# Moving adds and copies between engines in a pipelined Mamba block: D x and down's residual on TensorE, post-norm steps re-timed

## The chip, the cores and the metric

The kernel runs on one core of a Trainium2 chip. [...] An instruction waits at the head of its engine's queue until the semaphores that it names have come, and what is behind it waits too. Everything is 32-bit floating point. The metric is device time in microseconds (us) of one execution; lower is better.

## The reference

The input x has 4 sequences of 1024 rows of 256 values. Two layers follow each other, each with a layer norm in front and a residual sum behind it.

```
x = x + L0_attn(layernorm(x))      # a Mamba block with its own MLP
x = x + L0_ffn(layernorm(x))       # a gated FFN with a Walsh-Hadamard transform

L0_attn(h0):                                       # h0 = layernorm(x)
    z, x1, B, C, dt_raw = split(rmsnorm(h0) * n1 @ in_proj.T)  # 256, 64, 64, 256, 128 columns
    dt = softplus(dt_raw @ dt_proj.T + bias)
    state[g,p,n] = exp(dt*A) * state + (dt*x1) * B   # per time step: 256 rows (g,p), 32 states n
    y[g,p]       = sum_n state[g,p,n] * C[g,n]
    y = (y + D * x1) * silu(z)
    h = h0 + y @ out_proj.T
    return h + (silu(xn @ gate.T) * (xn @ up.T)) @ down.T      # xn = rmsnorm(h) * n2; 704 wide
L0_ffn(h1):                                        # h1 = layernorm(x after the first layer)
    return fwht(silu(h1 @ W1.T) * (h1 @ W3.T)) @ W2.T          # 1024 wide
```

## The kernel before

**Units and quarters.** The 4 x 1024 rows are cut into eight units of 512 rows (`T`), two to a sequence; unit 2k starts with an empty state ("even" units), unit 2k+1 goes on from the state that its predecessor left ("odd" units). For the scan, a unit has 256 rows x 32 states = 8192 recurrences over 512 time steps. They are worked on 128 partitions in 16 portions of four 512-long rows each, called q (0 to 127 over all units; `qs`, L696). For one q:

- SP issues `da` (dt copied over the states, 1 MB, L704 by `dma_da`) into one of four buffers, two halves of `ub` (dt*x1, 512 KB each), and for every second q `cr` (C, 256 KB);
- ACT turns da into exp(dt*A) in four instructions (`exp`, L741);
- DVE multiplies ub by B (`times_b`, L765, two instructions) and runs the recurrence (`scan`, L774, four instructions of 512 steps);
- POOL multiplies the states by C (`times_c`, L784, one instruction over 4 x 512; in even units it first copies the last state out, L783);
- PE sums over states (`sum_states`, L795, four matmuls) into the PSUM bank `py`, of which there is one; eight q fill it. Only then is the da buffer free, and the da of q+4 can be issued into it.

`pb`, a PSUM copy of B that times_b reads, is renewed every eight q by `copy_b` (L754).

**Ticks.** The order of every queue is written out by hand. Half a q is a tick; a unit is 32 ticks. `at(tick, lane, fn)` puts a step on a lane of a tick, and the loop at L858 records each tick's lanes in a fixed order: PE, ACT, times_b, ACTb, two exp of the next q, a scan, DVE, the other scan, POOL0, times_c, POOL, sum_states, PEend, ACTend, SP, the loads, SPend. No time is attached to a tick: it says only what stands ahead of what on each engine. "ACT" stands ahead of a tick's exponentials and "ACTend" behind them.

**What runs beside the scan.** `pre(u, H)` makes a unit's operands ahead of its first tick H: first norm (`row_stats`, `small`, `un`), transposes, the projection by `win` (x1/B, dt, C, z), and the DMAs that lay dt, dt*x1, C and x1 out in HBM. `post(u, E, other)` does the rest behind its last tick E: y = py + D x1 by DVE (`y_dx`, L810), times silu(z) by POOL (`y_z`, L815), out_proj (`add_rows`, L306), the second norm, the MLP's three pairs of products (`gated`, L245: matmuls, silu and `up` copies on ACT, product on POOL) and `down`, the third norm, the FFN's products and its output product with `w2h`. So while unit k is scanned, unit k-1 goes through `post` and unit k+1 through `pre`. Behind tick 256 there is no scan left, and the last units' `post` is all that runs (the tail).

`add_rows` adds a product to the residual `hr` in one of two ways: DVE adds PSUM to hr (L316: down's, and all three in the last unit), or ACT copies PSUM out (`evict`, L321) and POOL adds (L325: out_proj and w2h of the other units). `dense_psum` hands out four PSUM banks in turn to everything that is not py, pb or bx.

## Time and profile before

| what | us |
|---|---|
| median of 3 runs | 1163.14 (1161.78 to 1168.64) |
| the profiled execution: its own time | 1173.07 |
| its span on the core | 1171.2 |
| first scan begins, last scan ends | 22.07, 1053.61 |
| busy in that stretch (22 to 1053.6): DVE, PE, POOL, ACT | 949.4, 838.7, 839.0, 739.3 |
| behind it (1053.6 to 1171.2): PE, DVE, POOL, ACT | 104.1, 4.9, 36.1, 34.6 |
| share of the 16 DMA engines busy in the two | 0.87, 0.03 |

Times by unit, from the first scan of one to the first scan of the next, are 138.0, 126.4, 130.1, 128.2, 128.1, 128.6, 125.5 and (to the last scan's end) 126.6 us. The page of a profile gives busy times, a chain of work followed back from the end, and groups of instructions by source line; each idle time is put down to the semaphore that came last. A line such as L226 or L306 is that of a helper and serves several steps, which the names of the tiles tell apart (out<-in: `dense<-xt,w` is the FFN's first products, `dense<-ht,wg` the MLP's, `dense<-w2h,g` the output product). A 32-bit matmul stands in the trace as two records, so `x16` of L226 is eight matmuls of 512 columns.

### The profile page before, as it was taken

The page shows a single profiled execution, that of the slowest core. Times are in us where ns is not written, and L with a number is a line of the kernel's source. Part 1 is how long each engine was busy: PE and PEld are TensorE (multiplying, and loading weights), DVE is VectorE, ACT ScalarE, POOL GpSimd, SP SyncE. Part 2 cuts the span into 40 slices and gives each one's busy share as a digit, 9 for nine tenths or more (in the row PEclk, how much of TensorE's full clock was granted, in tenths as well). Part 3 has the DMA queues.
Part 4 walks back from the last instruction along what each step waited for, and adds up shares of the span by engine and source line. Part 5 has one row for each costly group of instructions (what it writes and reads, how often), then busy time and mean ns, then how long its engine had stood idle before and what let it go on. Part 6 is the DMA issues. An engine that isn't in the chain of part 4 may idle for free.

```text
span 1171.2 us, 11883 instructions
## 1 busy us (share of the span) xinstructions
PE 959.6 (82%) x3374; PEld 456.5 (39%) x3374; DVE 962.9 (82%) x840; ACT 782.2 (67%) x1411; POOL 887.1 (76%) x515
## 2 busy tenths in 40 slices
PE   8464236969998799969996999979997987799978
PEld 3121012423634255423633364424543362336535
DVE  4897799999998989999999899999999899990000
ACT  3835556868768786779677786878685967563331
POOL 6675758878978888878977998789977898674312
PEclk9777558979899799979998899979997999789989
DMA  7989999898799889997799889988799789730000
GB/s 252 352 300 351 353 327 308 311 325 296 250 340 320 300 298 320 319 327 281 270 348 325 281 300 334 319 325 297 270 310 360 281 291 343 262 111 1 18 0 18
DMA packets 89441, 321.89 MB, mean 275 GB/s; under 512 B 9312, under 2 KB 20000, under 8 KB 73120
## 3 DMA queue, kind: packets, MB, share of 16 engines
q1 hardware_dynamic: 87520, 318.38, 77.1%
q10 hardware_dynamic: 1856, 2.75, 0.7%
q8 instruction: 27, 0.44, 0.1%
q14 instruction: 38, 0.31, 0.1%
HBM read 302.22 MB, written 18.87 MB: 274 GB/s over the span
## 4 chain that ended last, share of the span: by engine, by line
PE 25%; DMA 7%; DVE 6%; POOL 6%; issue 5%; ACT 4%; DVEq 0%; POOLq 0%; ACTq 0%; SPq 0%
PE dense L226 14%; PE dense L306 8%; DMA da<-dtd 5%; POOL da L784 4%; DVE da L774 3%; DVE bx L765 3%; PE py L795 3%; DMA ub<-ud 2%; ACT da L741 1%; POOL m L274 1%; POOL g L274 1%; DVE hr L316 0%; ACT up L270 0%; ACT L741 0%; ACT junk L173 0%
## 5 line engine op out<-in xcount | busy, mean ns | idle before, releaser
L784 POOL TENSOR_TENSOR da<-da,cr 128x2048 f32<-128x2048 f32 x128 | 580.0, 4531 | 86.8 <-DVE da L774 22.5
L741 ACT ACTIVATE da<-da,nega 128x512 f32<-128x512 f32 x508 | 334.4, 713 | 170.8 <-DMA da<-dtd 159.3
L774 DVE TENSOR_TENSOR_SCAN da<-da,carry,bx 128x512 f32<-128x512 f32 x256 | 315.7, 1268 | 20.0 <-DVE bx L765 7.6
L774 DVE TENSOR_TENSOR_SCAN da<-da,bx 128x512 f32<-128x512 f32 x256 | 300.2, 1209 | 37.0 <-ACT da L741 21.3
L765 DVE TENSOR_TENSOR bx<-ub,pb 128x1024 f32<-128x1024 f32 x254 | 312.2, 1229 | 20.3 <-ACT pb L754 9.3
L795 PE MATMUL py<-da,rsel 128*32 128x512 f32 x1024 | 162.5, 712 | 159.4 <-POOL da L784 159.4
L226 PE MATMUL dense<-xt,w 128*128 128x512 f32 x512 | 238.4, 621 | 1.4 <-ACT si L263 1.4
L226 PEld LDWEIGHTS dense<-xt,w 128*128 128x128 f32 x512 | 99.4, 199 | 145.9 <-issue 123.4
L795 PEld LDWEIGHTS py<-da,rsel 128*32 128x32 f32 x1024 | 21.4, 115 | 243.0 <-POOL da L784 201.2
L306 PE MATMUL dense<-w2h,g 128*128 128x256 f32 x512 | 113.4, 380 | 0.0
L274 POOL TENSOR_TENSOR g<-si,up 128x512 f32<-128x512 f32 x64 | 80.5, 1272 | 32.3 <-ACT up L270 32.2
L306 PEld LDWEIGHTS dense<-w2h,g 128*128 128x128 f32 x512 | 96.8, 190 | 18.4 <-ACT ev L321 2.5
L306 PE MATMUL dense<-wd,m 128*128 128x256 f32 (+1 forms) x384 | 98.2, 400 | 0.9 <-POOL m L274 0.9
L316 DVE TENSOR_TENSOR hr<-hr,dense 128x512 f32<-128x512 f32 x20 | 13.4, 669 | 99.9 <-PE dense L306 99.9
L226 PE MATMUL dense<-ut,win 128*128 128x512 f32 x192 | 94.7, 625 | 0.2 <-ACT ut L220 0.2
L270 ACT COPY up<-dense 128x512 f32<-128x512 f32 x112 | 63.4, 579 | 46.8 <-PE dense L226 46.4
L274 POOL TENSOR_TENSOR m<-si,up 128x512 f32<-128x512 f32 (+1 forms) x48 | 60.2, 1270 | 43.5 <-ACT up L270 43.5
L226 PE MATMUL dense<-ht,wg 128*128 128x512 f32 x192 | 87.7, 600 | 3.4 <-ACT ht L220 3.4
L306 PEld LDWEIGHTS dense<-wd,m 128*128 128x128 f32 (+1 forms) x384 | 68.6, 192 | 37.6 <-issue 20.6
L263 ACT ACTIVATE si<-dense 128x512 f32<-128x512 f32 x112 | 60.7, 596 | 28.4 <-PE dense L226 25.5
L226 PE MATMUL dense<-ht,wu 128*128 128x512 f32 x160 | 72.8, 600 | 4.8 <-ACT si L263 4.8
L741 ACT ACT_TABLE_LOAD x44 | 56.5, 1283 | 4.8 <-DMA da<-dtd 4.0
(95 smaller groups left out, 798.6 us busy)
## 6 DMA issues: line engine op xcount, KB each, us to landing
da<-dtd SPq DMA_DIRECT2D x127, 1024.0 KB
ub<-ud SPq DMA_DIRECT2D x254, 512.0 KB
cr<-cd SPq DMA_DIRECT2D x64, 256.0 KB
x<-in_x SPq DMA_DIRECT2D x8, 512.0 KB
dtd<-dt SPq DMA_DIRECT2D x16, 256.0 KB
ud<-du SPq DMA_DIRECT2D x16, 256.0 KB
cd<-cc SPq DMA_DIRECT2D x16, 256.0 KB
out<-hr SPq DMA_DIRECT2D x8, 512.0 KB
```

The lines of the kernel that those rows point to most:

```text
L226: nc.tensor.matmul(dst[:n], lhsT=w[:, k, col : col + n], rhs=src[:, k, :], start=(k == 0), stop=(k == 1),)
L263: nc.scalar.activation(g[i]["si"][:n], g[i]["pg"][:n], AF.Silu)
L270: nc.scalar.copy(g[i]["up"][:n], g[i]["pu"][:n])
L274: nc.gpsimd.tensor_tensor(u[dst][:n, c, :], g[i]["si"][:n], g[i]["up"][:n], ALU.mult)
L306: nc.tensor.matmul(po[t // 2][:, t % 2, :], lhsT=left[k][:, t * P : (t + 1) * P], rhs=right[k], start=(k == 0), stop=(k == n - 1),)
L316: nc.vector.tensor_tensor(hr, hr, po[i], ALU.add)
L741: nc.scalar.activation(da, da if q else s["u"]["pdt", b], AF.Exp, scale=an[:, s["h"], s["j"], b, s["g"] : s["g"] + 1],)
L765: nc.vector.tensor_tensor(s["bx"], s["ub", b0 // 2], u["pb"].unsqueeze(1).broadcast_to([P, 2, T]), ALU.mult)
L774: nc.vector.tensor_tensor_scan(da, da, s["bx"][:, b % 2, :], start, ALU.mult, ALU.add)
L784: nc.gpsimd.tensor_tensor(s["da"], s["da"], s["cr"].unsqueeze(1).broadcast_to([P, 4, T]), ALU.mult)
L795: nc.tensor.matmul(u["py"][32 * b : 32 * b + 32, :], lhsT=rsel[:, 2 * s["j"] + s["g"], :], rhs=s["da"][:, b, :], start=first, stop=last,)
```

## The change

- **D x on TensorE.** `diagonal` makes two 128x128 diagonal matrices of D (`dd`, by ACT, once). `sum_states` starts each py with a matmul of dd and x1's rows (`xr`), 16 in all. `y_dx` on DVE becomes a copy of py by ACT, behind the exponentials of the same tick (ACTend); for the last half of the last unit DVE multiplies py by silu(z) straight away (`y_z_last`).
- **The rows behind down on TensorE.** `add_rows` with way "pe" starts each of down's four row blocks with a matmul of the identity and hr (32 in all); the sum is then copied back over hr by ACT (in the last unit, the second half by DVE) where DVE added it. Unit 6's out_proj, so far by ACT and POOL, goes the DVE way, and its w2h keeps POOL's.
- **copy_b** goes to ACT in 13 of 15 cases (7 before); DVE keeps q = 8 and 120.
- **Steps moved.** In units 0 to 5 all of `post` from the second norm's `hn` on is a tick later (F = E+1), and the third norm's `hn` stands behind the exponentials. In units 6 and 7 it is sooner: 2 ticks for the second norm and the MLP's first products (F = E-2), 3 to 5 for down and its statistics, 5 behind the third norm. `down` runs two row blocks to a tick there. Unit 6's four w2h blocks are at E+32, E+36 and twice E+50, which is, on PE's queue, ahead of unit 7's out_proj, behind it, and behind unit 7's down. In `pre`, `un` and the transposes are two ticks later (units 2 to 7), and the x1, dt and first C projections with the DMAs of x1 and B one tick later (units 1 to 7).
- **gated**: where z's matmul rides along, the first `up` copy stands behind the exponentials and the first product a tick later.
- **The end**: the last times_c is cut in two, the first half a tick sooner; unit 7's m and g lie in da's buffers instead of the one "big" buffer; the last half of its statistics is DVE's (`row_stats_vector`); its rows are stored in two halves.

```diff
     rsel = load("rsel", [P, 8, 32], a["rsel"])
+    dd = wp.tile([P, 2, P], F32, tag="dd", name="dd")
+    def diagonal(h):
+        nc.scalar.activation(dd[:, h, :], ident, AF.Identity, scale=dpar[:, h : h + 1])
...
-    def row_stats_first(u, src):
-        u["mv"] = sm.tile([P, 2, TT], F32, tag="mv", name="mv")
-        st = sm.tile([P, TT, 6], F32, tag="st", name="st")
-        ag = sm.tile([P, TT, 2], F32, tag="ag", name="ag")
-        for t in range(TT):
+    def row_stats_vector(u, name, ts=range(TT)):
+        src = u[name]
+        if 0 in ts:
+            u["mv"] = sm.tile([P, 2, TT], F32, tag="mv", name="mv")
+        st = p1.tile([P, TT, 6], F32, tag="st", name="st")
+        ag = p1.tile([P, TT, 2], F32, tag="ag", name="ag")
+        for t in ts:
             nc.vector.bn_stats(st[:, t, :], src[:, t, :])
-        for t in range(TT):
+        for t in ts:
             nc.vector.bn_aggr(ag[:, t, :], st[:, t, :])
-        nc.vector.tensor_copy(u["mv"][:, 1, :], ag[:, :, 1])
-        nc.vector.tensor_scalar(u["mv"][:, 0, :], ag[:, :, 0], -1.0 / 16, None, ALU.mult)
+        ts = slice(ts[0], TT)
+        nc.vector.tensor_copy(u["mv"][:, 1, ts], ag[:, ts, 1])
+        nc.vector.tensor_scalar(u["mv"][:, 0, ts], ag[:, ts, 0], -1.0 / 16, None, ALU.mult)
...
             c, n = chunks[i]
-            nc.gpsimd.tensor_tensor(u[dst][:n, c, :], g[i]["si"][:n], g[i]["up"][:n], ALU.mult)
+            nc.gpsimd.tensor_tensor(u[dst][c][:n], g[i]["si"][:n], g[i]["up"][:n], ALU.mult)
...
         at(tick + 1, "ACTend" if three else "ACT", silus)
-        at(tick + 2, "ACT", up, 0)
+        at(tick + 2, "ACTend" if z else "ACT", up, 0)
...
                 at(tick + 2, "ACTend", up, i)
-        at(tick + 2, "POOL", product, 0)
+        at(tick + 3 if z else tick + 2, "POOL", product, 0)
...
             at(tick + 3, "POOL", product, i)
-    def add_rows(tick, u, lhs, rhs, per_tick, lane="PE", on_pool=False):
+    def add_rows(ticks, u, lhs, rhs, lane="PE", way=None):
...
             n = len(left)
+            dst = po[t // 2][:, t % 2, :]
+            if way == "pe":
+                rows = u["hr"][:, t, :]
+                nc.tensor.matmul(dst, lhsT=ident, rhs=rows, start=True, stop=False)
...
                 nc.tensor.matmul(
-                    po[t // 2][:, t % 2, :],
+                    dst,
...
                     rhs=right[k],
-                    start=(k == 0),
+                    start=(k == 0 and way != "pe"),
...
             nc.vector.tensor_tensor(hr, hr, po[i], ALU.add)
+        def replace(i):
+            copy = nc.vector.tensor_copy if by_vector(i) else nc.scalar.copy
+            copy(u["hr"][:, 2 * i : 2 * i + 2, :], po[i])
+        def by_vector(i):
+            return u is us[-1] and i
...
         for t in range(TT):
-            at(tick + t // per_tick, lane, pe, t)
+            at(ticks[t], lane, pe, t)
             if t % 2:
-                after = tick + t // per_tick + 1
-                if on_pool:
+                after = ticks[t] + 1
+                if way == "pe":
+                    at(after, "DVE" if by_vector(t // 2) else "ACTend", replace, t // 2)
+                elif way == "pool":
...
             at(H - 54, "SP", load_x, u)
-            at(H - 45, "ACTend", lambda: row_stats(u, u["x"], (0, 1)))
-            at(H - 43, "ACTend", lambda: row_stats(u, u["x"], (2, 3)))
+            at(H - 45, "ACTend", row_stats, u, "x", (0, 1))
+            at(H - 43, "ACTend", row_stats, u, "x", (2, 3))
...
             at(H - 37, "POOL", small_end)
-            at(H - 32, "ACT", un, (0, 1))
-            at(H - 31, "ACT", un, (2, 3))
-            at(H - 30, "PE", lambda: transposes(u, s["un"]))
-            at(H - 30, "ACTend", transposed, u, "ut")
-        at(H - 24, "PE", pe_x)
-        at(H - 23, "ACT", act_x)
-        at(H - 22, "SP", dma_xb)
-        at(H - 19, "SPend", dma_xr, 0)
-        at(H - 17, "SPend", dma_xr, 1)
-        at(H - 16, "PE", pe_dt)
-        at(H - 16, "PE", pe_c, 0)
+            at(H - 30, "ACT", un, (0, 1))
+            at(H - 29, "ACT", un, (2, 3))
+            at(H - 28, "PE", lambda: transposes(u, s["un"]))
+            at(H - 28, "ACTend", transposed, u, "ut")
+        at(H - 23, "PE", pe_x)
+        at(H - 22, "ACT", act_x)
+        at(H - 21, "SP", dma_xb)
+        at(H - 18, "SPend", dma_xr, 0)
+        at(H - 16, "SPend", dma_xr, 1)
+        at(H - 15, "PE", pe_dt)
+        at(H - 15, "PE", pe_c, 0)
...
         s = {}
+        last = u is us[-1]
+        many = us.index(u) < len(us) - 2
...
         def big(name):
-            u[name] = p1.tile([P, 8, T], F32, tag="big", name=name)
-        def store():
-            b, c = u["b"], u["c"]
+            if last:
+                tiles = [pda.tile([P, 4, T], F32, tag="da", name=name) for _ in range(2)]
+                u[name] = [tiles[c // 4][:, c % 4, :] for c in range(8)]
+            else:
+                tile = p1.tile([P, 8, T], F32, tag="big", name=name)
+                u[name] = [tile[:, c, :] for c in range(8)]
+        def store(lo=0, n=TT):
+            b, first = u["b"], u["c"] * T + lo * P
             nc.sync.dma_start(
-                out=out[b, c * T : (c + 1) * T, :].rearrange("(t p) d -> p t d", p=P), in_=u["hr"]
+                out=out[b, first : first + n * P, :].rearrange("(t p) d -> p t d", p=P),
+                in_=u["hr"][:, lo : lo + n, :],
...
         add_rows(
-            E + 3,
+            (E + 3,) * TT,
...
             lambda: [W["wo"][:, k, :] for k in range(2)],
-            4,
             "PEend",
-            on_pool=u is not us[-1],
+            way="pool" if many else None,
         )
-        at(E + 5, "ACTend", lambda: row_stats(u, u["hr"], (0, 1), False))
-        at(E + 6, "ACTend", lambda: row_stats(u, u["hr"], (2, 3), False))
-        at(E + 7, "POOL", small2)
-        at(E + 8, "ACT", hn, "r3", None)
-        at(E + 9, "PE", lambda: transposes(u, s["tok"]))
-        at(E + 9, "ACTend", transposed, u, "ht")
-        at(E + 9, "POOL", lambda: nc.gpsimd.tensor_tensor(u["hr"], u["hr"], u["x"], ALU.add))
-        at(E + 10, "PE", big, "m")
+        for i in range(2):
+            at(E + (5 + i if many else 4), "ACTend", row_stats, u, "hr", (2 * i, 2 * i + 1), False)
+        F = E + 1 if many else E - 2
+        at(E + 7 if many else E + 5, "POOL", small2)
+        at(F + 8, "ACT", hn, "r3", None)
+        at(F + 9, "PE", lambda: transposes(u, s["tok"]))
+        at(F + 9, "ACTend", transposed, u, "ht")
+        at(F + 9, "POOL", lambda: nc.gpsimd.tensor_tensor(u["hr"], u["hr"], u["x"], ALU.add))
+        at(F + 10, "PE", big, "m")
...
         for i in range(2):
-            gated(E + 10 + 3 * i, u, "m", "wg", "wu", chunks[3 * i : 3 * i + 3], "ht",
+            gated(F + 10 + 3 * i, u, "m", "wg", "wu", chunks[3 * i : 3 * i + 3], "ht",
                   (other, i) if other else None)
+        down = (18, 19, 20, 21) if many else (17, 17, 18, 18)
         add_rows(
-            E + 18,
+            [F + t for t in down],
             u,
-            lambda: [u["m"][:n, c, :] for c, n in enumerate(sizes)],
+            lambda: [u["m"][c][:n] for c, n in enumerate(sizes)],
             lambda: [W["wd"][:n, c, :] for c, n in enumerate(sizes)],
-            1,
+            way="pe",
         )
-        at(E + 20, "ACTend", lambda: row_stats(u, u["hr"], (0, 1)))
-        at(E + 22, "ACTend", lambda: row_stats(u, u["hr"], (2, 3)))
-        at(E + 23, "POOL", small3)
-        at(E + 24, "ACT", hn, "r4", "nm")
-        at(E + 25, "PE", lambda: transposes(u, s["tok"]))
-        at(E + 25, "ACTend", transposed, u, "xt")
-        at(E + 26, "PE", big, "g")
+        at(F + down[1] + 1, "ACTend", row_stats, u, "hr", (0, 1))
+        if last:
+            at(F + down[3] + 1, "DVE", row_stats_vector, u, "hr", (2, 3))
+        else:
+            at(F + down[3] + 1, "ACTend", row_stats, u, "hr", (2, 3))
+        at(F + down[3] + 2, "POOL", small3)
+        if not many:
+            F -= 3
+        at(F + 24, "ACTend" if many else "ACT", hn, "r4", "nm")
+        at(F + 25, "PE", lambda: transposes(u, s["tok"]))
+        at(F + 25, "ACTend", transposed, u, "xt")
+        at(F + 26, "PE", big, "g")
...
         for i in range(3):
-            gated(E + 26 + 3 * i, u, "g", "w1", "w3", chunks8[3 * i : 3 * i + 3], "xt")
+            gated(F + 26 + 3 * i, u, "g", "w1", "w3", chunks8[3 * i : 3 * i + 3], "xt")
+        o2 = (E + 32, E + 36, E + 50, E + 50) if not (many or last) else range(F + 36, F + 40)
         add_rows(
-            E + 36,
+            o2,
             u,
-            lambda: [u["g"][:, c, :] for c in range(8)],
+            lambda: u["g"],
             lambda: [w2h[:, c, :] for c in range(8)],
-            1,
-            on_pool=u is not us[-1],
+            way=None if last else "pool",
         )
-        at(E + 43, "SPend", store)
+        if last:
+            at(o2[1] + 1, "SPend", store, 0, 2)
+            at(o2[3] + 1, "SPend", store, 2, 2)
+        else:
+            at(o2[3] + 4, "SPend", store)
...
         return s["u"]["carry"][:, s["h"], s["j"], :, s["g"]]
+    def by_vector(q):
+        return q in (8, NQ - 8)
...
         u["pb"] = ps_b.tile([P, T], F32, tag="b", name="pb")
-        (nc.vector.tensor_copy if h else nc.scalar.copy)(u["pb"], u["br", h])
+        (nc.vector.tensor_copy if by_vector(q) else nc.scalar.copy)(u["pb"], u["br", h])
...
         nc.vector.tensor_tensor_scan(da, da, s["bx"][:, b % 2, :], start, ALU.mult, ALU.add)
-    def times_c(q):
+    def times_c(q, parts=(slice(0, 4),)):
...
             nc.gpsimd.tensor_copy(carry_of(s), s["da"][:, :, T - 1])
-        nc.gpsimd.tensor_tensor(
-            s["da"], s["da"], s["cr"].unsqueeze(1).broadcast_to([P, 4, T]), ALU.mult
-        )
+        for part in parts:
+            da = s["da"][:, part, :]
+            n = da.shape[1]
+            nc.gpsimd.tensor_tensor(
+                da, da, s["cr"].unsqueeze(1).broadcast_to([P, n, T]), ALU.mult
+            )
...
             u["py"] = ps_y.tile([P, T], F32, tag="y", name="py")
+            x = u["xr"][:, s["h"], :]
+            nc.tensor.matmul(u["py"], lhsT=dd[:, s["h"], :], rhs=x, start=True, stop=False)
...
                 rhs=s["da"][:, b, :],
-                start=first,
+                start=False,
...
         if last:
-            at(2 * q + 4, "DVE", y_dx, u, s["h"])
-            at(2 * q + 5, "POOL0", y_z, u, s["h"])
-    def y_dx(u, h):
+            if q == NQ - 1:
+                at(2 * q + 4, "DVE", y_z_last, u)
+            else:
+                at(2 * q + 4, "ACTend", y, u, s["h"])
+                at(2 * q + 5, "POOL0", y_z, u, s["h"])
+    def y(u, h):
...
             u["yt"] = p3.tile([P, 2, T], F32, tag="T", name="yt")
-        nc.vector.scalar_tensor_tensor(
-            u["yt"][:, h, :], u["xr"][:, h, :], dpar[:, h : h + 1], u["py"], ALU.mult, ALU.add
-        )
+        nc.scalar.copy(u["yt"][:, h, :], u["py"])
...
         nc.gpsimd.tensor_tensor(u["yt"][:, h, :], u["yt"][:, h, :], u["zs"][:, h, :], ALU.mult)
+    def y_z_last(u):
+        nc.vector.tensor_tensor(u["yt"][:, 1, :], u["py"], u["zs"][:, 1, :], ALU.mult)
...
     at(-17, "ACTend", weights_ready)
+    for h in range(2):
+        at(1, "ACTend", diagonal, h)
...
         at(2 * q - 8, "SPend", dma_br, q)
-        at(2 * q - 1, "DVE" if q // 8 % 2 else "ACTb", copy_b, q)
+        at(2 * q - 1, "DVE" if by_vector(q) else "ACTb", copy_b, q)
...
         run(tick, "POOL0")
-        if half == 0 and has(q - 1):
+        if half == 0 and has(q - 1) and q < NQ:
             times_c(q - 1)
+        elif q in (NQ - 1, NQ) and tick >= 2 * NQ - 1:
+            if tick <= 2 * NQ:
+                times_c(NQ - 1, (slice(0, 2) if half else slice(2, 4),))
```

## The prediction

> **What bounds the kernel now.** I read the page's first part, then busy times by stretch, then VectorE's queue in order of time, then the waits, then the tail. First the page, and the two stretches into which the last scan cuts the span (columns: length, busy us and instructions of each engine, granted clock of TensorE, share of the DMA engines, GB/s).

> ```profile
> span 1171.2 us, 11883 instructions
> ...
> PE 959.6 (82%) x3374; PEld 456.5 (39%) x3374; DVE 962.9 (82%) x840; ACT 782.2 (67%) x1411; POOL 887.1 (76%) x515
> ...
> 22.00:1053.60 1031.60, 838.70 (x2993) 386.78 (x2995) 949.38 (x805) 739.28 (x1326) 839.01 (x460) 0.89 0.87 306
> 1053.60:1171.20 117.60, 104.14 (x348) 62.10 (x340) 4.89 (x8) 34.63 (x75) 36.05 (x29) 0.97 0.03 9
> ```

> While scans run, DVE is busy 949 of 1032 us; behind them it is idle and TensorE works 104 of 118 us. These are two regimes and I add them up apart. That DVE sets the pace of the first shows in its queue, here two ticks of unit 7:

> ```profile
> 1006.35 1.23 DVE L765 TENSOR_TENSOR bx<-ub,pb 128x1024 f32<-128x1024 f32 x1
> 1007.67 1.28 DVE L774 TENSOR_TENSOR_SCAN da<-da,carry,bx 128x512 f32<-128x512 f32 x1
> 1008.87 0.66 DVE L316 TENSOR_TENSOR hr<-hr,dense 128x512 f32<-128x512 f32 x1
> 1009.44 1.27 DVE L774 TENSOR_TENSOR_SCAN da<-da,carry,bx 128x512 f32<-128x512 f32 x1
> 1010.75 1.23 DVE L765 TENSOR_TENSOR bx<-ub,pb 128x1024 f32<-128x1024 f32 x1
> 1012.09 2.45 DVE L774 TENSOR_TENSOR_SCAN da<-da,carry,bx 128x512 f32<-128x512 f32 x2
> 1014.57 1.23 DVE L765 TENSOR_TENSOR bx<-ub,pb 128x1024 f32<-128x1024 f32 x1
> ```

> No line names a wait. The tick with an add takes 4.40 us, the next 3.82: an add costs the scan 0.58, its 0.66 less some overlap. But the others are close, as units 2 (even) and 3 (odd) show:

> ```profile
> 286.50:416.60 130.10, 115.42 (x407) 56.01 (x406) 117.16 (x101) 96.88 (x177) 109.74 (x70) 0.91 0.87 300
> 416.60:544.80 128.20, 116.67 (x427) 55.24 (x427) 120.96 (x101) 100.42 (x183) 109.04 (x54) 0.95 0.89 314
> ```

> DVE is busy 117 and 121 us, PE 115 and 117. An even unit has shorter scans (1209 ns against 1268 with a carry), so there the rest must hurry, and there DVE loses 13 us. Where it waits, and what SP waits for:

> ```profile
> DVE hr L316 <- PE dense L306: 99.9, 6, 43.9
> ...
> DVE yt L810 <- PE py L795: 12.5, 7, 8.9
> ...
> DVE bx L765 <- ACT pb L754: 9.3, 3, 4.1
> ...
> SPq L704 <- PE py L795: 286.2, 95, 7.3
> ```

> The first is nearly all tail, as is 8.9 us of the second. The fourth is the ring: the da of q+4 is issued when PE has summed q, so a late PE delays an exponential four q on. In unit 2 the margin between exponential and scan falls from 9.7 us (q 32) to nothing (q 39).

> **DVE's work that goes (scan stretch).** y_dx: 15 of the 16 stand there, at 733 ns less the same 0.09 overlap: 15 x 0.64 = 9.6, and 12.5 - 8.9 = 3.6 of waiting for py, which moves to ACT. copy_b: 6 at 674 ns, 6 x 0.58 = 3.5. Adds: 14 of down go, 2 for unit 6's out_proj come: 12 x 0.58 = 7.0. **Sum 23.7 us.**

> **A stall that should go.** At the end of units 2, 4 and 6 DVE waits 9.3 us for pb. ACT's queue tells why (unit 2's end):

> ```profile
> 412.38 0.60 ACT L263 ACTIVATE si<-dense 128x512 f32<-128x512 f32 x1 [0.63 <-PE dense L226]
> 414.09 0.58 ACT L270 COPY up<-dense 128x512 f32<-128x512 f32 x1 [1.11 <-PE dense L226]
> 414.58 0.60 ACT L754 COPY pb<-br 128x512 f32<-128x512 f32 x1
> ```

> pb stands behind silu and an up copy of the FFN's second product group, which wait for a late PE. A tick later (F = E+1) both stand behind pb. What is late next is PE's first group; the gain lies between 0 and 9.3, I take **6**, since one group less stands ahead of it.

> **TensorE's additional work.** The FFN's 512-column matmuls run at 16 records in 7.13 us, 0.89 for a matmul; the 256-column ones of w2h at 64 records in 13.98, 0.44. So 16 x 0.89 + 32 x 0.44 = 28.3 us, 26.5 of it in the scan stretch, 3.5 a unit: PE 119 to 120 us against a unit of some 124. It is free where PE waits for POOL ahead of py (159.4 us in all in the group of L795) and goes into the ring where PE is behind. The first matmul of a py also waits until ACT has emptied the one bank. Today py of q 48 could start when its times_c ended at 427.7; the exponentials of q 50, behind which the copy will stand, began at 427.4, so with 1.33 for two, 0.58 and 0.89 it starts at 430.2, 2.5 late; at q 40 it is 0.6, at q 120 nothing. ACT gets 15 + 15 + 6 copies of 0.58 = 21 us more, in 28 to 33 us of idle time a unit. Against all this, the first `up` copy no longer holds exponentials (at 337.34 it waited 2.13 us for PE, and DVE then 0.70 for da), and the later product frees POOL. The net cost is bounded by nothing and by the even units' whole share of the 23.7, about 10; I take **6**, nearer to the second, because at q 39 the margin is zero.

> [...]

> [...]

> **Edits at nothing.** dd: two ACT instructions at tick 1, in waits for the first da. The DMAs of x1 and B, with pe_x, act_x and pe_dt, move a tick behind da's issues on SP; they keep their distance of three ticks to each other, and make_u reads x1 five ticks (19 us) after its issue instead of six; without that cover u would be late, up to a tick (3.8 us) a unit. `un` two ticks later still has five ticks to pe_x. Four more ACT table loads of 1283 ns go under ACT's idle time. Unit 6's two adds by DVE, at its tick 4, stand ahead of a scan: out_proj has a tick for its 3.5 us.

> **The tail.** PE's queue today:

> ```profile
> 1061.31 1.06 PE L795 MATMUL py<-da,rsel 128*32 128x512 f32 x8
> ...
> 1064.66 3.29 PE L306 MATMUL dense<-wo,yt 128*128 128x256 f32 x14 [1.66 <-POOL yt L815]
> 1067.79 13.98 PE L306 MATMUL dense<-w2h,g 128*128 128x256 f32 x64
> 1081.60 1.04 PE L213 MATMUL dense<-ident,hn 128*128 128x128 f32 x8
> ```

> The last scan ends at 1053.61, out_proj runs at 1064.66. In between the last times_c ends at 1058.4, and py waits behind unit 6's FFN until 1061.3. Changed, POOL is free at 1052.2; two halves at 2.36 (the 128x1024 add of L659) end at 1057.0; unit 6's FFN is long done; py 1.06, y_z_last 0.75: out_proj at 1059.0. **5.6 less.** From there to the MLP's first matmul (1082.93) it is 18.3 us, because 14 us of w2h stand ahead of the transposes. Now one block of 3.5 does: out_proj 3.5, add 0.7, two statistics 1.2, r3 on POOL 1.35, hn 2.0, transposes and copy 1.3, one evict ahead of hn 0.6, gaps 0.2: 10.9. **7.4 less.** Down has four identity matmuls more, the first in a wait for POOL: **1.3 more.** Behind down PE idles today from 1115.0 to the FFN at 1123.5; unit 6's last two blocks (7.1) and the transposes (1.3) take that place, so VectorE's statistics gain nothing. Sum **11.7 us less**; the evict and the final store leave about 2 either way.

> **The sum.** 23.7 + 6 - 6 + 11.7 = 35.4. The profiled execution took 1173.07, so 1137.7; the median of the runs is 9.9 below it, and **1128 us** is the forecast, 1118 to 1138 with the terms' bounds.

> **Rivals.** (1) The ring decides in even units: what DVE saves there comes back as waits for exponentials, and pb's stall too. Then the odd units' share stays: 8 x 0.64, 3.2 of waiting, 3 copies and 6 adds at 0.58, 13.5, with the tail 25.2: 1138, up to 1146. For it: the margin at q 39; against it: up and product no longer in front. (2) Freeing ACT and POOL undoes the even units' stalls altogether: 23.7 + 9.3 + 3 (the wait at 355.3 in unit 2) + 11.7: 1115. Against it: PE's 3.5 us a unit. (3) PE becomes the bound everywhere: its 26.5 come in full, 23.7 + 6 - 26.5 + 11.7 = 15: 1148, or 1158 if half of ACT's 21 us adds to it; that is the case in which the change does little. Against it: 7 us of PE waiting for POOL in unit 2 alone. (4) **Slower**: the hand-over of py. The copy stands behind exponentials that wait for a da landing, some 10 us after its issue (issued at 392.7, used at 403.2); if ACT loses its lead, PE's whole queue stands at dd's matmul, da is issued late, and ACT is later still. At 2.4 us in each of 15 places it eats the 35 us; from 3.2 on the kernel is slower by over 1%; at 5 it is 1203. Against it: today's rows give 0 to 2.5.

> **How the numbers follow.** Forecast 0.58, (1) 0.18, (2) 0.10, (3) 0.07, of which 0.04 within 1%, (4) 0.07. Faster by over 1% (11.6 us; less than that a measurement can hardly tell from no change): 0.58 + 0.18 + 0.10 + 0.03 = 0.89; same 0.04; slower 0.07. The range 1112 to 1148 leaves out (4), most of (3), and the best of (2).

> **What would show it.** Right: no L810, DVE ticks of 3.7 to 3.95 throughout; no wait for pb at the ends of units 2, 4 and 6; units of 122 to 126 us; some 106 us behind the last scan. PE busy near 120 a unit with scans waiting for da is (1) or (3); PE waiting for an ACT copy of py is (4). I am wrong above all if the even units stay at 128 to 130.

## The result and the profile after

| | us |
|---|---|
| changed kernel, median of 10 runs | 1173.27 (1168.95 to 1176.45) |
| kernel before, beside it, median of 10 runs | 1165.37 (1158.28 to 1169.44) |
| ratio | 1.0066, 95% interval 1.0040 to 1.0092 |
| forecast | 1128 (1112 to 1148) |

The changed kernel is 0.7% slower, where 35 us less were forecast. Its profiled execution took 1169.56 us. First its page, then its two stretches (columns as before: length, busy us and instructions of TensorE (PE), its weight loads (PEld), VectorE (DVE), ScalarE (ACT) and GpSimd (POOL), granted clock, DMA share, GB/s; SP, in other rows, is SyncE, which issues DMAs):

```profile
span 1167.6 us, 12110 instructions
...
PE 984.9 (84%) x3470; PEld 472.8 (40%) x3470; DVE 942.3 (81%) x812; ACT 805.2 (69%) x1443; POOL 883.7 (76%) x513
```

```profile
22.50:1061.20 1038.70, 869.06 (x3101) 404.35 (x3099) 928.34 (x772) 767.26 (x1372) 841.56 (x463) 0.90 0.84 304
1061.20:1167.60 106.40, 99.80 (x336) 60.98 (x332) 5.34 (x12) 29.66 (x60) 30.04 (x26) 0.97 0.03 10
```

Behind the last scan it is 11.2 us shorter, as forecast. While scans run, VectorE has 21.0 us less to do (949.38 to 928.34), and yet the stretch is 7.1 us **longer**: its idle time grew by 28. Units take 136.8, 123.8, 129.6, 131.3, 128.0, 130.1, 128.6 and 130.5 us.

The 7.1 is rather too small: the profiled execution of before lies 7.7 us above the median of its ten runs, that of after 3.7 below, and medians 7.9 us apart with a tail 11.2 us shorter leave some 19 us for the stretch. Units 0 and 2 of before's profile, 138.0 and 130.1 us, seem to hold that surplus: e12 of the table below has the order of before in these units, and there they take 134.3 and 126.1. A difference of 2 to 4 us in a single unit can therefore be spread between executions.

The waits say for what VectorE idles (columns: total, times, longest); first of the kernel before, then of the changed one:

```profile
DVE da L774 <- ACT da L741: 21.5, 18, 4.2
```

```profile
DVE da L824 <- ACT da L787: 39.1, 34, 4.2
DVE bx L815 <- ACT pb L804: 18.1, 8, 3.2
DVE hr L331 <- PE dense L321: 4.9, 2, 3.8
```

Scans wait for exponentials 18 us more, and pb, 9.3 us before at the ends of three units, now costs 18.1, of which 15.7 lie in the middle of units 2 to 6. With 4.9 us for unit 6's adds (the last row, from the scans' stretch alone), less the 3.6 for py that are gone, that is nearly all of the growth of the idle time. The timeline of unit 3 shows how pb comes late:

```profile
476.28 0.58 ACT L280 COPY up<-dense 128x512 f32<-128x512 f32 x1 [1.69 <-PE dense L236]
...
478.00 0.58 ACT L804 COPY pb<-br 128x512 f32<-128x512 f32 x1
...
478.62 1.23 DVE L815 TENSOR_TENSOR bx<-ub,pb 128x1024 f32<-128x1024 f32 x1 [3.10 <-ACT pb L804]
```

pb's copy, now ACT's, stands behind an up copy that waits for a late TensorE, and two exponentials. It is the stall of the unit ends over again, at another tick. And unit 6's two adds, priced at nothing, stop the scans in unit 7:

```profile
949.27 3.72 PE L321 MATMUL dense<-wo,yt 128*128 128x256 f32 x16
...
951.37 0.69 DVE L331 TENSOR_TENSOR hr<-hr,dense 128x512 f32<-128x512 f32 x1 [3.85 <-PE dense L321]
...
953.10 0.69 DVE L331 TENSOR_TENSOR hr<-hr,dense 128x512 f32<-128x512 f32 x1 [1.04 <-PE dense L321]
```

From the end of the scan ahead of them to the start of the next that is 6.2 us, 4.9 of them waiting, for what was to have a tick of room.

**The loop.** From the issue of a da to the issue of the one four q later, which uses the same buffer, I added up the steps in each trace (unit 3, means, us):

| | issue to first exp | to first scan | scans | to times_c | times_c | to the end of py | to the next issue | sum |
|---|---|---|---|---|---|---|---|---|
| before | 9.68 | 6.93 | 6.53 | 0.37 | 4.53 | 3.15 | 0.36 | 31.6 |
| after | 9.10 | 3.66 | 6.49 | 2.74 | 4.53 | 5.77 | 0.17 | 32.5 |

Without a wait, four q of an odd unit take VectorE 31.0 us (4 x 7.76, its tick pairs without stalls), of an even one 30.1. Before, odd units ran at 31.6 (units 3 and 5) and even ones at 31.9 to 33.1; after, units 2 to 6 all run at 32.3 to 32.6. The sum itself is four times the step from q to q, whatever sets it. What tells is the margin between the first exponential and the first scan: in the odd units before, it was 6.8 to 6.9 us, and no scan of unit 3 waited for an exponential, so there VectorE itself set the pace. After, it is 3.7 in unit 3 and has gone into lags behind the scan, on POOL and TensorE.

These are means. In unit 3 after, 13 of the 15 steps from one q's first scan to the next take 7.73 to 8.36 us, near VectorE's own 7.76; two, at q 55 and q 57, take 12.14 and 9.73. Before, five took 8.1 to 8.3, one 9.46 and the others 7.73 to 7.77. So the work that was removed does show, and a few new stalls cost more.

### The profile page after: what moved, and what is told of

Read it like the earlier page. It is cut to its first block, busy times and chain, and to the rows that moved or that the text cites. A ratio compares the mean times of both kernels' runs of the same rounds, so it can differ in the third digit from the quotient of the medians.

```text
span 1167.6 us, 12110 instructions
## 1 busy us (share of the span) xinstructions
PE 984.9 (84%) x3470; PEld 472.8 (40%) x3470; DVE 942.3 (81%) x812; ACT 805.2 (69%) x1443; POOL 883.7 (76%) x513
## 4 chain that ended last, share of the span: by engine, by line
PE 52%; DMA 17%; ACT 13%; POOL 10%; issue 4%; DVE 4%; SPq 0%; DVEq 0%; POOLq 0%; ACTq 0%
PE dense L236 29%; PE dense L321 14%; DMA da<-dtd 11%; POOL da L837 7%; PE py L850 6%; ACT da L787 5%; DMA cr<-cd 3%; DVE da L824 2%; DVE bx L815 1%; ACT L787 1%; PE dense L319 1%; ACT up L280 1%; DMA w<-in_w 1%; ACT L273 1%; ACT si L273 1%
## 5 line engine op out<-in xcount | busy, mean ns | idle before, releaser
L815 DVE TENSOR_TENSOR bx<-ub,pb 128x1024 f32<-128x1024 f32 x254 | 312.2, 1229 | 29.5 <-ACT pb L804 18.1
L236 PE MATMUL dense<-xt,w 128*128 128x512 f32 x512 | 242.9, 628 | 22.5 <-ACT xt L230 22.5
L850 PE MATMUL py<-da,rsel 128*32 128x512 f32 x1024 | 152.4, 670 | 92.1 <-POOL da L837 91.9
L321 PE MATMUL dense<-w2h,g 128*128 128x256 f32 x512 | 117.4, 386 | 1.2 <-ACT ut L230 1.2
L321 PEld LDWEIGHTS dense<-w2h,g 128*128 128x128 f32 x512 | 96.7, 192 | 27.5 <-issue 12.5
L236 PE MATMUL dense<-ht,wg 128*128 128x512 f32 x192 | 90.6, 617 | 5.3 <-ACT ht L230 5.3
L321 PEld LDWEIGHTS dense<-wd,m 128*128 128x128 f32 (+1 forms) x384 | 71.2, 192 | 23.9 <-issue 9.9
L787 ACT ACT_TABLE_LOAD x46 | 59.0, 1283 | 0.7
L236 PEld LDWEIGHTS dense<-ut,win 128*128 128x128 f32 x192 | 37.1, 199 | 52.9 <-issue 49.5
```

What stands on the lines that cost most here:

```text
L236: nc.tensor.matmul(dst[:n], lhsT=w[:, k, col : col + n], rhs=src[:, k, :], start=(k == 0), stop=(k == 1),)
L321: nc.tensor.matmul(dst, lhsT=left[k][:, t * P : (t + 1) * P], rhs=right[k], start=(k == 0 and way != "pe"), stop=(k == n - 1),)
L787: nc.scalar.activation(da, da if q else s["u"]["pdt", b], AF.Exp, scale=an[:, s["h"], s["j"], b, s["g"] : s["g"] + 1],)
L815: nc.vector.tensor_tensor(s["bx"], s["ub", b0 // 2], u["pb"].unsqueeze(1).broadcast_to([P, 2, T]), ALU.mult)
L850: nc.tensor.matmul(u["py"][32 * b : 32 * b + 32, :], lhsT=rsel[:, 2 * s["j"] + s["g"], :], rhs=s["da"][:, b, :], start=False, stop=last,)
```

## The experiments

Times are medians of 4 to 10 runs; each ratio is to the kernel before on the same chip, with its 95% interval. The intervals are 0.2 to 0.4% wide on either side, so two kernels less than some 4 us apart are not told apart. "Half clock" adds up the records of TensorE's granted clock at 0.5 from the first scan of unit 2 to the last scan.

| kernel | us | ratio | half clock, us |
|---|---|---|---|
| before | 1163.5 to 1166.6 | 1 | 109 |
| after | 1173.3 | 1.0066 (1.0040, 1.0092) | 82 |
| e1: after, pb's copies as before | 1172.5 | 1.0053 (1.0024, 1.0081) | 89 |
| e2: after, down's adds on VectorE | 1176.6 | 1.0096 (1.0059, 1.0133) | 99 |
| e3: after, D x on VectorE | 1167.8 | 1.0014 (0.9989, 1.0039) | 99 |
| e4: after without TensorE's adds | 1170.8 | 1.0022 (0.9993, 1.0051) | 113 |
| e5: after, gated as before | 1186.8 | 1.0175 (1.0148, 1.0202) | 99 |
| e6: after, ticks as before | 1166.0 | 0.9995 (0.9966, 1.0023) | 106 |
| e7: e5 and e6 together | 1170.3 | 1.0039 (1.0017, 1.0061) | 109 |
| e12: before with the tail's part alone | 1155.7 | 0.9917 (0.9885, 0.9949) | 99 |
| e8: after, half of ub's transfers | 1155.2 | 0.9900 (0.9880, 0.9920) | 79 |
| e10: e8 with a fifth da buffer | 1126.0 | 0.9669 (0.9639, 0.9699) | 58 |
| e9: after, half of W3 | 1164.1 | 0.9983 (0.9962, 1.0004) | 116 |
| e17: after, useless matmuls | 1158.3 | 0.9947 (0.9919, 0.9975) | 17 |
| e11: after, xt by VectorE | **1154.4** | 0.9913 (0.9884, 0.9942) | 61 |
| e13: e11, D x on VectorE | 1166.5 | 1.0011 (0.9986, 1.0036) | 96 |
| e14: e11, ticks as before | 1168.2 | 1.0028 (0.9999, 1.0057) | 113 |
| e15: before, xt by VectorE | 1168.8 | 1.0041 (1.0018, 1.0064) | 106 |
| e16: e12, xt by VectorE | 1159.5 | 0.9951 (0.9928, 0.9974) | 113 |
| e18: e11 and e17 together | 1156.8 | 0.9928 (0.9903, 0.9953) | 17 |

### One move at a time

e1, pb's copies:

```diff
-        return q in (8, NQ - 8)
+        return q // 8 % 2 == 1
```

> The changed kernel with copy_b as before: DVE renews pb in every odd half of a unit, ACT in the others. In the changed kernel DVE waits 18.1 us for the copies on ACT, 15.7 of it in tick 15 of units 2 to 6. Theory A (the work moved to ACT stands in line behind waits, and DVE waits for it directly): those 15.7 us go, 3.5 come back as DVE's own copies, so about 12 us less than the changed kernel, 1161. Theory B (the ring of four da buffers, made late by TensorE, sets the pace, and any stall of DVE only uses up slack): the waits move to the exponentials, within 4 us of the changed kernel's 1173.

The waits for pb go, those for exponentials rise from 39.1 to 59.2 us, and the time stays (Theory B): the stall only changes its name.

e2, down's adds in units 0 to 6:

```diff
-            way="pe",
+            way="pe" if last else None,
```

> The changed kernel with down's residual added by DVE again in units 0 to 6 (the last unit keeps the identity matmuls): 28 identity matmuls (12.3 us of TensorE) and 14 ACT copies (8 us) go, 14 DVE adds (8 us) come. Theory A: DVE's 8 us show, less waits of ACT, about 1173 to 1179. Theory B: TensorE is earlier by 1.8 us a unit, the waits for exponentials shrink by about as much as DVE gets, 1165 to 1173.

No gain, if anything a loss.

e3, D x (the last half unit keeps dd):

```diff
-        nc.scalar.copy(u["yt"][:, h, :], u["py"])
+        nc.vector.scalar_tensor_tensor(
+            u["yt"][:, h, :], u["xr"][:, h, :], dpar[:, h : h + 1], u["py"], ALU.mult, ALU.add
+        )
```

> The changed kernel with D x on DVE again for all but the very last half unit: 15 diagonal matmuls (13.4 us of TensorE) and 15 copies of py by ACT (8.7 us) go, 15 DVE instructions (9.6 us and some waiting for py) come. Theory A: the copies of py by ACT are part of the waits at ticks 18 and 3 to 4, about 1168 to 1176. Theory B: TensorE is earlier by 1.8 us a unit and py's bank is free sooner, 1163 to 1170.

5.4 us less than after, though VectorE has more to do: the hand-over of py costs something, net a third of a microsecond at each half unit.

e4, no matmuls of dd and of the identity, so that D x and the rows behind down are missing from its sums:

```diff
-            nc.tensor.matmul(u["py"], lhsT=dd[:, s["h"], :], rhs=x, start=True, stop=False)
...
-                nc.tensor.matmul(dst, lhsT=ident, rhs=rows, start=True, stop=False)
```

> The changed kernel without the additional matmuls: D x and the residual behind down are left out of the result, everything else stays, ACT's copies too. Theory B: TensorE's 28.3 us are what takes the gain back, so 15 to 28 us less than the changed kernel, 1145 to 1158. Theory A: TensorE is not what DVE waits for, 0 to 8 us less, 1165 to 1173.

28 us of matmuls taken away give 2.5 us, which is not clear of noise. TensorE's additional work as such is not what took the gain. But look at its clock: 113 us at half, where after has 82. I come back to that.

### The order, and the tail alone

e5, gated's old places:

```diff
-        at(tick + 2, "ACTend" if z else "ACT", up, 0)
+        at(tick + 2, "ACT", up, 0)
...
-        at(tick + 3 if z else tick + 2, "POOL", product, 0)
+        at(tick + 2, "POOL", product, 0)
```

> gated's first up copy and first product go back to their old places (up ahead of the tick's exponentials, product at tick+2); all else as in the changed kernel. Theory R (four da buffers, held by queues that work in order, set a pace of some 32.4 us for four q whatever one engine is relieved of): within 5 us of the changed kernel, POOL's waits for up (59 and 48 us for g and m) shrink to the old 32 and 43, waits for exponentials grow. Theory G (the later up and product delay POOL's times_c and that took the gain): some 15 to 25 us faster than the changed kernel, near 1150.

It is slower than either theory had it: the later up copy and product are worth 13.5 us with the new ticks, and 4.3 with the old ones (e6 against e7). e6, F and pre's ticks:

```diff
-        F = E + 1 if many else E - 2
+        F = E if many else E - 2
...
-            at(H - 30, "ACT", un, (0, 1))
+            at(H - 32, "ACT", un, (0, 1))
...
-        at(H - 23, "PE", pe_x)
+        at(H - 24, "PE", pe_x)
...
```

> The steps of units 0 to 5 behind the second norm go back to their old ticks (F = E), the third norm's hn ahead of the exponentials, and pre's steps to their old ticks; gated keeps the new places, units 6 and 7 and the moves between engines too. Theory R: within 5 us of the changed kernel. Theory S (the later steps crowd the end of a unit, where up, pb and y copies now stand in one ACT queue): 10 to 20 us faster than the changed kernel, the 3.1 us waits for pb in the middle of a unit gone, the 6 to 9 us ticks at the ends of units 2, 4 and 6 back.

> Both of the above at once: what remains of the change is the work moved to TensorE and ScalarE (D x, down's rows, pb) and the tail. If the moved work alone is worth what the forecast gave it (23.7 us of VectorE), about 1135 to 1145. Theory R: 1160 to 1172, since the tail's 11 us are all that is left of it. Theories G and S together: 1140.

The late ticks cost some 7 us, between the two theories of e6, and e7 stays in the range of Theory R: the moved work alone is not worth the 23.7 us. e12 is e7 with e1, e2 and e3, that is the kernel before with the changes in units 6 and 7 and at the end:

> Of the change only what concerns units 6 and 7 and the end remains: their steps sooner, TensorE's adds in the last half unit, the split times_c, da's buffers for m and g. D x, down's adds and pb's copies of all units before are VectorE's again, gated and the ticks of units 0 to 5 and of pre as before. The tail measured 11.2 us shorter in the changed kernel: 1150 to 1157. If unit 6's two adds on VectorE (6.2 us of waiting in unit 7) and the units' own spread eat it: 1157 to 1163.

The tail alone gives its 10 us and is faster than both kernels. e7 and e12 differ by nothing but the moves between engines. Their scan stretches, e12 and then e7:

```profile
22.15:1050.69 1028.54, 845.57 (x3017) 390.28 (x3016) 950.84 (x807) 747.84 (x1337) 843.41 (x463) 0.90 0.87 307
```

```profile
21.91:1062.97 1041.06, 877.00 (x3101) 407.49 (x3099) 928.30 (x772) 766.98 (x1372) 842.40 (x463) 0.89 0.86 303
```

VectorE is relieved of 22.5 us and the stretch becomes 12.5 us longer (14.6 between the medians). This is the plainest measurement against my forecast. The waits from 282 to 1000 us of the two show the way; TensorE's for the copy of py and VectorE's for pb, e12 and then e7:

```profile
PE py L849 <- DVE yt L869: 4.2, 1, 4.2
DVE bx L815 <- ACT pb L804: 8.4, 3, 3.7
```

```profile
PE py L848 <- ACT yt L868: 17.9, 6, 3.5
DVE bx L815 <- ACT pb L804: 32.7, 8, 6.0
```

In e7 TensorE stands six times, up to 3.5 us, at the first matmul of a new py until ACT has copied the old one out; what is behind it in its queue comes later, and ACT's up copies and the pb copy behind them too. In the changed kernel, with the later ticks, the same wait is 6.4 us. That the hand-over of py is what makes the moves cost 14.6 us is read from these waits; e7 without it was not run.

### Transfers and buffers

e8, in `dma_ub`, and e10, which has the last two lines as well:

```diff
+        if half:
+            s["ub", 1] = s["ub", 0]
+            return
...
-    pda = ctx.enter_context(tc.tile_pool(name="pda", bufs=4))
-    pub = ctx.enter_context(tc.tile_pool(name="pub", bufs=6))
+    pda = ctx.enter_context(tc.tile_pool(name="pda", bufs=5))
+    pub = ctx.enter_context(tc.tile_pool(name="pub", bufs=4))
```

> The changed kernel with half of ub's transfers left out: the second half of each q uses the first half's rows of dt*x1, so the output is another; 127 transfers of 512 KB, some 65 of 318 MB, go, and every instruction of the engines stays. If the wait for da's landing (9.0 us from issue to the first exponential) is mostly transfers ahead of it in the one queue, it falls to 6 or 7 us, four q take 30 to 31 us in place of 32.4, and the kernel is 35 to 55 us faster than the changed one. If the loop is held by the engines' queues alone (exponentials behind copies, POOL behind products, py behind projections), within 10 us of the changed kernel.

> As the kernel with half of ub's transfers left out (1155.2 us), and the space that this frees is given to a fifth da buffer, so that da of q+5 waits for q. Theory R: the ring opens, four q take VectorE's own 30 to 31 us, units of 121 to 124 us, 1105 to 1115 us in all. Theory P: units stay near 128 and the kernel within 12 us of 1155, VectorE's waits for exponentials go and TensorE's lag behind times_c grows instead.

The DMA engines' share between 100 and 1000 us, after and then e8:

```profile
100.00:1000.00 900.00, 772.91 (x2781) 365.29 (x2782) 804.00 (x669) 673.53 (x1210) 739.66 (x402) 0.91 0.85 307
```

```profile
100.00:1000.00 900.00, 783.32 (x2830) 373.18 (x2826) 814.63 (x677) 674.25 (x1213) 744.88 (x401) 0.92 0.68 241
```

A fifth of the bytes less, and 18 us of gain, between the two cases of the expectation. The profiled executions differ by 15.7 us; 12.0 of them lie in unit 0 and 3.6 in unit 2, part of which can be spread. Units 3 to 7 take 129 to 131 us, as in after (128 to 131). Four q still take 32.4 to 32.5 there (units 3 to 6). With the fifth buffer (and the same bytes as e8) units 2 to 7 fall to 123.2, 125.1, 124.0, 125.0, 122.8 and 127.4, and four q to 30.9 to 31.2 us (units 2 to 6), close to VectorE's own pace; the kernel does not reach Theory R's 1105 to 1115, but is nearer to it than to Theory P's 1143 and more. So in the steady state, with half of ub's transfers, it is the number of da buffers, not the DMA engines' load, that holds the loop. ACT's waits from 282 to 1000 us, after, e8, and the longest that e10 still has:

```profile
ACT da L787 <- DMA da<-dtd: 56.2, 24, 4.9
```

```profile
ACT da L790 <- DMA da<-dtd: 57.7, 30, 4.8
```

```profile
ACT up L280 <- PE dense L236: 28.1, 24, 2.2
```

Among ACT's waits in e10 in that stretch there is none of an exponential for a landing. The fifth buffer takes the place of the ub that is left out here; with ub whole it was not tried.

### TensorE's work and TensorE's clock

e9, one contraction step of two for W3 in units 0 to 5:

```diff
+                cut = w == "w3" and us.index(u) < len(us) - 2
-                g[i][name] = project(W[w], c * P, n, u[src])
+                g[i][name] = project(W[w], c * P, n, u[src], None, range(1) if cut else range(2))
```

> The changed kernel with half of the FFN's second product (W3) left out in units 0 to 5: one of its two contraction steps, so the output is another; 8 matmuls of 512 columns a unit go from TensorE (8 x 0.89 = 7.1 us a unit, 43 us in all), nothing on the other engines. Theory P (TensorE's queue is the pace: from the FFN's first matmul to down it works without a gap, some 100 us of a unit, while the scan of the same steps needs 90; only the third norm gives it some 11 us of idle time): 30 to 43 us faster than the changed kernel, 1130 to 1143, units of 123 to 126 us. Theory R (the four da buffers, with copies and exponentials in one ACT queue and products and times_c in one POOL queue, hold the loop without TensorE): within 10 us of the changed kernel, TensorE's idle time grows by what is cut.

43 us less work, 9 us of gain, half clock up from 82 to 116 us. Theory P falls as it stood. What the clock does is seen if the third norm that runs during unit 3 is cut along the clock's records, here after (the column behind POOL's is the granted clock):

```profile
508.18:511.60 3.42, 3.42 (x19) 2.47 (x21) 3.28 (x4) 2.10 (x5) 0.41 (x1) 1.00 0.87 319
511.60:515.01 3.41, 0.88 (x8) 0.00 (x0) 3.21 (x3) 3.28 (x11) 3.23 (x1) 1.00 0.75 289
515.01:518.42 3.41, 1.94 (x8) 0.20 (x8) 3.27 (x4) 1.98 (x5) 3.00 (x6) 0.50 1.04 429
518.42:521.84 3.42, 2.76 (x8) 1.48 (x8) 3.19 (x3) 1.98 (x4) 3.09 (x5) 0.50 1.02 418
521.84:525.25 3.41, 0.14 (x1) 0.14 (x1) 3.27 (x4) 1.99 (x4) 3.24 (x3) 0.50 1.03 413
525.25:528.66 3.41, 3.41 (x4) 1.38 (x5) 3.17 (x4) 1.52 (x3) 2.95 (x4) 0.50 0.76 305
```

TensorE is busy 0.88 of the 3.41 us from 511.60, and the next window has half the clock. So have the three behind it, in all four with TensorE busy 1.94, 2.76, 0.14 and 3.41 us; from 528.66, behind the one of 3.41, the clock is 1.00 again. The FFN's first eight records, from 525.11 on, take 5.45 us where e17, at a granted clock of 1.00, needs 3.70. That the half clock is a cause was tested by adding work that nobody reads:

```diff
+            at(F + 23, "PE", busy, s, 3)
+            at(F + 25, "PE", busy, s, 1)
+            at(F + 25, "PEend", busy, s, 4)
...
+            nc.tensor.matmul(s["idle"], lhsT=ident, rhs=w2h[:, 0:2, :], start=True, stop=True)
```

> The changed kernel with eight matmuls a unit more in units 0 to 5, whose results nobody reads, in TensorE's waits at the third norm: three ahead of the second py behind down, one ahead of the transposes, four behind them (8 x 0.89 = 7.1 us a unit, 43 us of TensorE in all). Theory C (in windows of 3.41 us in which TensorE is less than about half busy it loses half its clock for the windows to come, and the FFN's first products then run at half speed on the path): the half-clock stretches of 13.7 us at the third norm shrink or go, each unit gains 2 to 4 us, 1148 to 1163. If the half clock only goes along with a late unit: no gain, and up to 43 us slower where the added matmuls outlast the waits, 1170 to 1216.

The windows of Theory C are those of the clock's records, 3.41 us each in the rows above; of the 19 in the trace of after that a half one followed, the busiest had TensorE busy for 60%.

43 us of TensorE's time added, 15 us of the kernel's gone (median; 11.3 between the profiled executions). The same place in e17:

```profile
504.65:508.07 3.42, 3.42 (x14) 1.06 (x6) 3.22 (x3) 3.29 (x11) 3.38 (x1) 1.00 0.99 337
508.07:511.48 3.41, 2.22 (x11) 0.45 (x10) 3.27 (x4) 2.00 (x4) 3.00 (x6) 1.00 1.03 425
511.48:514.89 3.41, 2.49 (x11) 1.44 (x12) 3.17 (x4) 1.85 (x4) 3.08 (x5) 1.00 1.04 419
514.89:518.31 3.42, 2.97 (x8) 1.19 (x7) 3.28 (x4) 2.13 (x4) 3.25 (x3) 1.00 1.01 406
```

```profile
518.04 3.70 PE L242 MATMUL dense<-xt,w 128*128 128x512 f32 x8 [0.45 <-ACT xt L236]
```

By these two traces the FFN's first eight records end 1.0 to 4.8 us sooner after the start of each of units 1 to 6, 15 us in all, but the six units together are only 4.9 us shorter, 3.5 of them in unit 2; the rest of the 11.3 lies in unit 0, which the edit does not touch, unit 7 and the tail. So the 2 to 4 us a unit of Theory C did not come in each unit, and how much of the 15 us the clock alone is worth stays open. The added matmuls also take one of the four PSUM banks that `dense_psum` hands out in turn, which was not tested apart.

The clock also goes some way to explain why e4 and e9 gained so little: what is taken from TensorE there makes it idle sooner, and the half clock lasts longer (113 and 116 us in place of 82; 17.1 us at the third norm in unit 3 of e4 in place of 13.7).

By an estimate of mine, half of the time at a granted clock of 0.50, the five stretches of 13.65 us in units 2 to 6 would cost 34 us if TensorE had work in all of it. e17 got at most 15 of them back; in the four half-clock windows above TensorE was busy for 8.25 of the 13.65 us and idle in the rest.

### The copy at the third norm

The chain of waits of after runs through this place (start, length, what):

```profile
512.65 10.52 DMA da<-dtd
...
523.26 1.33 ACT da L787 x2
524.59 0.48 ACT xt L230
...
525.11 5.45 PE dense L236 x8
530.56 1.00 PE py L850 x8
531.56 7.06 PE dense L236 x16
```

A da is issued late, ACT stands at its exponentials, xt stands behind them, and TensorE behind xt. e11 lets VectorE copy xt, which makes its own work 7 us more:

```diff
-        at(F + 25, "ACTend", transposed, u, "xt")
+        vec = (nc.vector.tensor_copy,) * 2
+        at(F + 25, "DVE" if many else "ACTend", transposed, u, "xt", *([vec] if many else []))
```

> The changed kernel with the two copies of the transposed third norm (xt, from PSUM) made by VectorE between two scans in units 0 to 5, where ACT makes them behind exponentials that wait for a da landing. Theory P: the FFN's first matmul comes up to 3 us sooner a unit (TensorE waited 3.33 us for xt in unit 3), all of it counts, since TensorE has no gap afterwards: 8 to 18 us faster, 1155 to 1165. Theory R: same or up to 8 us slower, by VectorE's additional 12 x 0.6 us.

19 us off the changed kernel; it beats both kernels and, narrowly, the range of Theory P. Was that place the bound before, too? e15 makes the same edit at E + 25 of the kernel before, e16 in e12:

> The kernel before with nothing but xt copied by VectorE in units 0 to 6. Theory H (the third norm's hand-over, xt behind exponentials that wait for a late da, stands on the path of both kernels): 10 to 20 us faster than before, 1146 to 1156, though VectorE has 14 x 0.6 us more to do. Theory A (only the change put it there, by its later ticks and fuller ACT queue; before it VectorE was the pace): 0 to 8 us slower than before.

> The kernel with only the tail's part of the change (1155.7) and xt copied by VectorE. Theory H: 1138 to 1147, faster than e11 by what the moves cost. Theory A: 1154 to 1162, and then the moves in e11, 1154.4, are worth what they lose elsewhere.

It was not: neither gains by the same edit (before loses 0.4%, e12's loss is not clear of noise), and Theory H falls for the kernel before. TensorE's waits from 282 to 1000 us say why; before, after, e11:

```profile
PE py L795 <- POOL da L784: 47.4, 31, 6.7
PE dense L213 <- ACT hn L200: 18.4, 5, 5.8
```

```profile
PE dense L236 <- ACT xt L230: 18.3, 5, 4.5
PE py L850 <- POOL da L837: 18.0, 5, 3.9
```

```profile
PE dense L236 <- DVE xt L230: 3.6, 5, 1.2
```

TensorE's queue of before, at the same third norm:

```profile
512.13 2.80 PE L213 MATMUL dense<-ident,hn 128*128 128x128 f32 x8 [1.56 <-ACT hn L200]
516.78 1.93 PE L795 MATMUL py<-da,rsel 128*32 128x512 f32 x8 [1.85 <-POOL da L784]
518.64 8.90 PE L226 MATMUL dense<-xt,w 128*128 128x512 f32 x16
```

With F = E the FFN's first product stands behind a py that waits for POOL; with F = E + 1 that py comes ahead of the transposes, and the FFN waits for xt alone. A step moved by one tick, costed at nothing, changed which wait ends last.

e14 is e11 with e6's edit, e13 e11 with e3's:

> xt copied by VectorE, and the old ticks of units 0 to 5 and of pre. Against e11 (1154.4): the old ticks alone gained 7 us on the changed kernel; if that was another way to the same hand-over, nothing is left of it (1152 to 1158); if it was their own place, 1147.

The old ticks take e11's gain away and more: 14 us slower than e11, outside both alternatives, and 2 slower than e6. That xt makes no difference there fits, for with the old ticks it is not waited for; TensorE then waits 26.3 us for hn and 17.9 for the copy of py (282 to 1000 us).

> xt copied by VectorE, and D x on VectorE as before the change (except the last half unit). Against e11 (1154.4): if the py bank's hand-over (matmul of dd waiting for ACT's copy) and the 0.9 us matmul still stand on the path, 5 us faster, about 1149; if VectorE's 9.6 us count now that the third norm's hand-over is gone, 5 to 10 us slower.

So does D x on VectorE, 12 us slower than e11 where 5 to 10 were expected at most, though it helped without e11. VectorE then waits 17.7 us for py (282 to 1000 us), and the half clock is back at 96 us; which of the two does it was not separated.

e18 has e11's edit and e17's, with two matmuls behind the transposes:

> The changed kernel with both edits: xt copied by VectorE (1154.4 alone) and useless matmuls in TensorE's waits at the third norm, three, one and two a unit (1158.3 alone with three, one and four). If the late xt and the half clock are two costs: some 10 us below e11, 1140 to 1148. If they are two ways to one place: 1150 to 1158.

The two edits do not add up: two ways to one place.

## Why the prediction was wrong

**The step that failed** is the net cost that I set against VectorE's removed work: "bounded by nothing and by the even units' whole share of the 23.7, about 10; I take 6". The work itself was right: 20.1 of the 23.7 us are work, and VectorE's busy time fell by 21.0. But its idle time grew by 28 us where I had it shrink by some 4, so the cost ate the whole gain and more; e7 against e12 has the moves at 14.6 us slower. The bound was none, because I took the odd units' gain as safe. That VectorE sets the pace was right for them as they stood (units 3 and 5 before), but not for what the change makes of them: copies of py and pb now stand in ACT's queue, TensorE waits for them and ACT for TensorE, and units 3 and 5 became slower, 128.2 and 128.5 us in e12 against 131.1 and 131.2 in e7. The even units 2, 4 and 6, at 129.6, 128.0 and 128.6, gave the sign that my last line names.

**The stall at the unit ends**: right, those ticks fell from 6.9, 7.9 and 5.8 us to 4.4 to 4.7, 7.1 us in all (6 forecast). I had the mechanism, pb behind up copies that wait for TensorE, and did not apply it to the pb copies that the change itself puts on ACT: 15.7 us in units 2 to 6, tick 15.

**Edits at nothing**: unit 6's adds cost 6.2 us, because TensorE reached out_proj late; the ticks cost some 7 us (e6), for which e11 and the waits point to xt on the path, though e6 moves F and pre's ticks together. gated's later copy and product, weighed as a relief, were one: 13.5 us (e5).

**The tail**: right, 11.2 us for 11.7, and 10 by e12.

**The rivals**: the first, the ring, had the mechanism; bound to the even units and with the odd units' share kept, it gave 1138. Neither its price nor any case from 1112 to 1148 let the loop become slower than before. The fourth, py's hand-over, had the right side and, in part, the right mechanism: on the changed kernel e3 puts it at 5.4 us net, not at the 36 that it needed, while with the old ticks (e7) TensorE waits 17.9 us for ACT's copy. TensorE's added matmuls, the third, cost 2.5 us net (e4), not clear of noise. Nothing at all, in place of the 6 that I took, would have been nearer, though not because TensorE had room: from the FFN's first product on, its matmuls follow each other in units 2 to 6 for 34 us and more without a gap of 0.2 us.

For what paces the scan stretch of the changed kernel, three edits each shorten it: a fifth da buffer (e10, 29 us beyond e8, with half of ub's transfers), xt taken out of ACT's queue, where it stands behind exponentials that wait for a landing (e11, 19 us), and matmuls that keep TensorE's clock up (e17, 15 us, not in addition). That these are links of one loop is argued from the waits, not shown link by link. Open is how the 14.6 us of the moves divide: one by one, taken back on the changed kernel, none is worth more than 5.4.

## What to carry to other kernels

Where buffers are handed round through several queues that work in order, write down the loop (issue, landing, each engine's lag, next issue) for several stretches before an engine's saved work is counted as time: an engine that is 92% busy and sets the pace can become the follower by the very move that relieves it. A step put on another queue inherits what stands ahead of it there, so look for the stall that you explain at every place to which the change moves the same step. When TensorE waits at one place in each round, look at the granted clock of the windows around it; here, taking 28 and 43 us of matmuls away gained 2.5 and 9 us (e4, e9), and 43 us of useless ones saved 15 (e17).

## What the runs showed of the hardware

The other surprise is how little a fifth of the DMA traffic matters once the first units are past (units 3 to 7 take 129 to 131 us at a share of 0.68 in e8, and 128 to 131 at 0.85 in after), and how much one more buffer does with the same bytes as e8 (123 to 127 in e10).
